# A cross-attention kernel whose hand-written statement order is replaced by another: first rounds, steady round and end

## The chip, the core and the metric

The kernel runs on one core of a Trainium2 chip. The core has a matrix engine (TensorE, PE in the profile, with its weight loads listed as PEld), a vector engine (VectorE, DVE), a scalar engine (ScalarE, ACT), a general engine (GpSimd, POOL) and a queue processor (SyncE, SP) that only issues DMAs here. Each engine takes its instructions in the order in which the program lists them and waits at one until the semaphores that it needs have come. The metric is the device time of one execution in microseconds. Three runs of the kernel before took 1341.26, 1343.85 and 1344.12 us, a median of 1343.85.

## The reference

64 blocks, each of 256 rows of text `x` (width 512) and 256 rows of audio `ctx` (width 384), in float32:

```python
text_p  = einsum('bld,dh->blh', H_l, W_text) + b_text
audio_p = einsum('bsd,dh->bsh', H_a, W_audio) + b_audio
Q = layer_norm(text_p, g1, beta1)
K = layer_norm(audio_p, g2, beta2)
V = audio_p
alpha = softmax(einsum('blh,bsh->bls', Q, K) / sqrt(512))
H_hyper = einsum('bls,bsh->blh', alpha, V)
H_hyper = einsum('blh,hk->blk', H_hyper, W_out) + b_out
return layer_norm(H_hyper + H_l, g_out, beta_out)
```

## The kernel before

All products are float32. To spend fewer products, the kernel uses fast schemes of the Strassen kind: the query projection (class `Fork`, methods `one` to `seven`, 7 products instead of 8), the key projection and the output projection (class `Thirds`, methods `one` to `five`, 15 products of 171 columns), the scores (`score_part`, 7 products) and the context (`z_part`, `context_two`). W_audio and W_out are multiplied together once (`fold_multiply`), so the context is taken over the raw audio rows. These schemes pay with sums of operands, which run on GpSimd and VectorE: `csum` of the audio side (`Sides.add`), `xsum` of the text side (`SumX.add`), `query_step`, `key_step`, `c_step`, `e_step` and `z_step`, and with additions between two products on the accumulators in PSUM (`start_t`, `start_l0`, `start_l1`, `take_m`, `start_u`, `middle_v` and their like on VectorE; `copy_n1`, `copy_t`, `copy_n`, `copy_u`, `after_one`, `after_seven` on ScalarE). A product that needs such a step has to wait for it.

PE contracts over partitions, so operands must be transposed. The kernel transposes 32x32 squares on VectorE (`turn`, line 76, and line 520). For that a matrix is fetched from HBM so that each 32-row strip lies where the transposition wants it: `squares` (line 73) issues four DMAs on SP. x and ctx come from the inputs (`load_x`, `load_c`); normalised queries, keys and the softmax weights are written to a scratch in HBM first (`store` and `store_e`, lines 498 and 931) and fetched back as squares (`fetch` and `fetch_e`), then turned (`turn`, `turn_e`). So each fetch of squares stands between a store and a transposition.

The 64 blocks go through a software pipeline. In round b of the loop, `k2` and `q2` are the key and query projection of block b+2, `at` is the attention of block b (affine of queries and keys, scores, softmax), `last` is the context of block b-1, `old` with `y = old.o` is the output projection of block b-2, `settled` is the final layer norm of block b-3, `cT[b+3]` and `xT[b+3]` are the transposed inputs of block b+3 with their sums, and the loads are for block b+4. The loop runs for b from 3 to 60. Before it stand the first rounds, written out statement by statement with the weights' preparation between them (`third_weights`, `weight_sums`, `turn_weights`, `fold_multiply`), and behind it the end, written out as well, in which the last blocks use plain products (`score`, `context_one`, `multiply`, `multiply_halves`) and the last layer norm is done in halves.

There is no scheduler: `tc.manual_schedule()` leaves the instructions in the order of the statements, which sets the order on every engine's queue and on SP's. Tiles with one buffer (`once`: `kr`, `qr`, `qsum`, `ksum`, `zsum`, `esum`, `asum`, the rooms `n1`, `t`, `m`, `n`, `u`, `d`) and the PSUM banks (`ps_m`, `ps_l`, `ps_u`, `ps_n` for Thirds, two `ps_f` for Fork, two rotating `at` banks for scores and contexts) are written again in each round.

This is the round before (the conditions on b at the last blocks are left out, and the lines that only name things):

```python
k2 = k[b + 2] = Thirds("k", b + 2, cs.pop(b + 2), wa_blocks, ba_sb, ba_delta); old.copy_two(); old.product_sums(); y = old.o; old.z_step(0);
q2.seven(); at.affine_queries(1); old.z_step(7); old.z_step(1); k2.one(); k2.copy_n1(); k2.start_t(); at.affine_queries(0); at.query_sums();
at.query_step(0); load_c(b + 4); q2.six(); at.open_scores(); k2.two(); q2.after_seven(); k2.three(); q2.start_q3(); at.score_part(1, 7); k2.copy_t();
last.fetch_e(); q2.step_r(); k2.start_l1(); k2.start_l0(); q2.five(); old.z_step(2); cT[b + 3] = turn_c(b + 3); at.affine_queries(3); k2.four();
settled.totals(); settled.deviation(0); settled.deviation(1); k[b + 1].turn([0]); settled.last_deviation(); at.copy_p7(); k2.take_m(); k2.start_u();
k2.five(); q2.after_five(); at.affine_queries(2); last.context_sums(); last.c_step(0); q2.four(); at.copy_p1(); settled.shift(1); k2.copy_n();
old.z_step(3); last.c_step(1); k2.copy_u(); k2.leave_ends(); old.z_step(4); cs[b + 3] = Sides(cT.pop(b + 3), "csum").add(0); cs[b + 3].add(1); cs[b +
3].add(1); y.seed(); k2.middle_v(); q2.square(var[:, :2], [1]); k2.leave_middle(); k2.middle_less(); at.query_step(1); old.z_step(5); last.turn_e();
q2.two(); y.one(); settled.shift(0); at.query_step(2); at.score_part(6); k2.leave(); k2.square(var[:, 2:], [1]); y.copy_n1(); old.z_step(6);
q2.three(); y.start_t(); at.add_p7(0); done.store(); done = settled; xT[b + 3] = turn_x(b + 3); y.three(); at.score_part(5); last.weight_sums();
last.e_step(0); last.open_context(); last.z_part(7); at.query_step(3); k2.square(var[:, 2:], [0]); last.e_step(1); y.two(); at.add_p7(1);
at.score_part(2); q2.square(var[:, :2], [0]); cs[b + 3].add(1); y.copy_t(); scales_of(q2, k2, var); at.score_part(3); k[b + 1].turn([1]);
y.start_l1(); last.keep_z7(); q2.normalise([0]); q2.normalise([1]); y.start_l0(); load_x_rows(b - 1); Fork.seed(); last.z_part(1); y.four(); q[b +
1].turn(); x_new = SumX(xT.pop(b + 3)); x_new.add(1); load_c_rows(b); k2.normalise([1]); at.score_part(4); last.e_step(2); settled.settle(1);
last.copy_z1(); k2.normalise([0]); x_new.add(1); last.c_step(2); y.take_m(); last.z_part(6); y.start_u(); att[b + 1] = Attention(b + 1); att[b +
1].affine_keys(0); at.maxima(); y.five(); last.c_step(3); last.add_u3(); cs[b + 3].add(1); settled.settle(0); last.z_part(5); att[b +
1].affine_keys(2); x_new.add(1); load_x(b + 4); last.add_c22(); q3 = q[b + 3] = Fork(b + 3, x_new.of, wt_blocks); q3.one(); x_new.add(1); att[b +
1].affine_keys(1); cs[b + 3].add(1); last.z_part(3); at.exponentials([0]); cs[b + 3].add(1); y.plus_middle(x_old, 1); last.z_part(4);
at.exponentials([1]); y.plus_ends(x_old); q2.store(); y.plus_n0(); att[b + 1].affine_keys(3); at.reciprocals(); att[b + 1].key_sums(); att[b +
1].key_step(0); k2.store(); last.context_two(0); y.last_11(); last.z_part(2); k2.seed(); at.divide_e([0]); q2.fetch(); at.divide_e([1]);
y.plus_middle(x_old, 0); last.copy_top(); y.last_10(); last.context_two(1); k2.fetch(); cs[b + 3].add(1); att[b + 1].key_step(1); y.last_01(x_old);
at.store_e(); last.add_c21(); y.last_00(); q3.after_one(); att[b + 1].key_step(2)
```

Of the kernel before, what the change touches and what calls it, by code (L numbers as in the profile page):

```python
# [22 lines left out]
def kernel(  # L23
# [1289 lines left out]
    war = []  # L1313
    pool, tag = (once, 'e')
    war.append(pool.tile([P, HC, P], F32, tag=tag, name=f'war_{0}'))
    arrange(war[0], wa_sb[:, 0, :], HC, nc.gpsimd.tensor_copy)
# [5 lines left out]
    k[0].multiply(0, [0])  # L1322
    mean_wa = means(wa_sb, AC, 'mwa')
    k[0].multiply(1, [0])
    k[0].multiply(0, [1])
    k[0].multiply(0, [2])
    pool, tag = (work, 'eT')
    war.append(pool.tile([P, HC, P], F32, tag=tag, name=f'war_{1}'))
    arrange(war[1], wa_sb[:, 1, :], HC, nc.gpsimd.tensor_copy)
    pool, tag = (work, 'eT')  # L1330
    war.append(pool.tile([P, HC, P], F32, tag=tag, name=f'war_{2}'))
    arrange(war[2], wa_sb[:, 2, :], HC, nc.gpsimd.tensor_copy)
    x_turn = RowTurn(x_0, DC, 'xT')
    x_turn.tile(0)
    k[0].multiply(1, [1])
    k[0].multiply(1, [2])
    x_turn.tile(1)
    mean_wt = means(wt_sb, DC, 'mwt')
    centre(wa_sb, mean_wa, AC)
    wa_t = const.tile([P, 11, WP], F32, tag='wa_thirds', name='wa_thirds')  # L1340
    third_weights(wa_sb, wa_t, [1], nc.vector)
# [3 lines left out]
    k[0].evict(0)  # L1345
    bt_row = bt_sb.rearrange('p (o h) -> p o h', o=1)
    mean_bt = means(bt_row, 1, 'mbt')
    k[0].evict(1)
    q[0].multiply(1, [0])
    q[0].multiply(1, [1])  # L1350
    q[0].multiply(0, [2])
    cT[1] = turn_c(1)
    q[0].multiply(0, [3])
    q[0].multiply(1, [2])
    q[0].multiply(1, [3])
    centre(bt_row, mean_bt, 1)
    third_weights(wa_sb, wa_t, [0])
    wa_blocks = third_weights(wa_sb, wa_t, [3])
    k[0].scales()
    centre(wt_sb, mean_wt, DC)  # L1360
    k[0].normalise([0])
    k[1] = Projection('k', 1, cT.pop(1), wa_sb, ba_sb, AC, ST, bank[4:6])
    k[1].multiply(0, [0])
    turn_weights(0, 1)
    turn_weights(1, 1)
    xT[1] = turn_x(1)
    q[0].evict(0)
    q[0].evict(1)
    wt_blocks = weight_sums(wt_sb, DC // 2, 'wtsum')
    k[1].multiply(0, [1])  # L1370
    k[1].multiply(0, [2])
    turn_weights(2, 1)
    q[0].scales()
    k[0].normalise([1])
    k[1].multiply(1, [0])
    k[1].multiply(1, [1])
    ba_row = ba_sb.rearrange('p (o h) -> p o h', o=1)
    mean_ba = means(ba_row, 1, 'mba')
    centre(ba_row, mean_ba, 1)
    xs_1 = SumX(xT.pop(1), nc.vector)  # L1380
    xs_1.add(1)
    turn_weights(3, 1)
    fold_multiply(1, 0, 1)
    third_weights(wa_sb, wa_t, [4], nc.vector)
    fold_multiply(0, 0, 1)
    g1_sb, be1_sb, g2_sb, be2_sb, bac_sb = take_columns()
    k[1].multiply(1, [2])
    k[0].store()
    folds.append(p_at.tile([P, H], F32, tag='at', name='ps_fold'))
    fold_multiply(2, 0, 1)  # L1390
    ba_delta = third_bias(ba_sb, 'ba_delta')
    q[0].normalise([0])
    k[1].evict(0)
    Fork.seed()
    fold_multiply(1, 1, 2)
    k[1].evict(1)
    load_c(2)
    fold_multiply(0, 1, 2)
# [3 lines left out]
    q[1].one()  # L1402
    xs_1.add(1)
    bt_step = const.tile([P, H2], F32, tag='bt_step', name='bt_step')
    nc.vector.tensor_tensor(bt_step, bt_sb[:, :H2], bt_sb[:, H2:], ALU.subtract)
    xs_1.add(1)
    load_c(3)
    q[1].seven()
    load_x(2)
    cT[2] = turn_c(2)  # L1410
    k[1].square()
    bias_rest(part, 1, 2)
    k[1].scales()
    fold_multiply(0, 2, 3)
    cs[2] = Sides(cT.pop(2), 'csum')
    cs[2].add(1)
    q[1].after_one()
    q[1].after_seven()
    cs[2].add(1)
    q[1].six()  # L1420
    cs[2].add(1)
    cs[2].add(1)
    q[0].normalise([1])
    q[1].start_q3()
    fold_multiply(0, 3, 4)
    q[1].step_r()
    q[0].store()
    xs_1.add(1)
    fold_multiply(1, 2, 3)
    k[0].fetch()  # L1430
    fold_evict(0)
    q[0].fetch()
    q[1].five()
    load_x(3)
    Thirds.seed_with(ba_sb)
    k[1].normalise([0])
    k[1].normalise([1])
    q[1].after_five()
    cs[2].add(1)
    bias_rest(part, 2, 3)  # L1440
    nc.vector.tensor_scalar(be2_sb, be2_sb, scale, None, ALU.mult)
    cs[2].add(1)
    cs[2].add(1)
    fold_multiply(1, 3, 4)
    bias_rest(part, 3, 4)
    k2_0 = k[2] = Thirds('k', 2, cs.pop(2), wa_blocks, ba_sb, ba_delta)
    k2_0.one()
    k2_0.copy_n1()
    q[1].two()
    k[1].store()  # L1450
    third_weights(wa_sb, wa_t, [2], nc.vector)
    q[1].three()
    k2_0.start_t()
    q[1].four()
# [370 lines left out]
    for b in range(3, B - 3):  # L1825
# [21 lines left out]
        if b + 4 < B: load_c(b + 4)  # L1847
# [503 lines left out]
```

## Time and profile before

| | |
|---|---|
| runs | 1341.26, 1343.85, 1344.12 us |
| profiled execution, own time | 1341.63 us |
| its span, first to last instruction | 1339.8 us |
| instructions | 29994 |
| granted clock of TensorE | 0.999 |
| PE busy | 1329.2 us, 99% |
| DVE busy | 1227.5 us, 92% |
| ACT busy | 1166.9 us, 87% |
| POOL busy | 1152.9 us, 86% |
| DMA | 322.24 MB, mean 241 GB/s |

The span is what the trace covers, and the own time is that of the same execution as the runs are timed, 1.8 us more. A product on PE is listed with the time from its start until its modelled end, while the next one starts earlier, so the distance between starts tells more than the listed time. An entry in brackets behind a row is the engine's idle time before it and what ended it. "SPq" rows are DMA issues; the time is that of the issue, not of the transfer. The chain of work that ended last goes back from the last instruction, at each step to what released it.

### The profile page before, as it was taken

The page shows a single profiled execution, that of the slowest core. Times are in us where ns is not written, and L with a number is a line of the kernel's source. Part 1 is how long each engine was busy: PE and PEld are TensorE (multiplying, and loading weights), DVE is VectorE, ACT ScalarE, POOL GpSimd, SP SyncE. Part 2 cuts the span into 40 slices and gives each one's busy share as a digit, 9 for nine tenths or more (in the row PEclk, how much of TensorE's full clock was granted, in tenths as well). Part 3 has the DMA queues.
Part 4 walks back from the last instruction along what each step waited for, and adds up shares of the span by engine and source line. Part 5 has one row for each costly group of instructions (what it writes and reads, how often), then busy time and mean ns, then how long its engine had stood idle before and what let it go on. Part 6 is the DMA issues. An engine that isn't in the chain of part 4 may idle for free.

```text
span 1339.8 us, 29994 instructions
## 1 busy us (share of the span) xinstructions
PE 1329.2 (99%) x8473; PEld 1246.9 (93%) x8473; DVE 1227.5 (92%) x3308; ACT 1166.9 (87%) x3304; POOL 1152.9 (86%) x1838
## 2 busy tenths in 40 slices
PE   9999999999999999999999999999999999999997
PEld 5899999999999999999999999999999999999996
DVE  6669999999999999999999999999999999999968
ACT  5888888898898888998898898988988988888885
POOL 5768899998998988998998999989989989888854
PEclk9999999999999999999999999999999999999999
DMA  9999898889899888998999888998988898988773
GB/s 213 239 247 237 239 257 242 246 248 243 240 260 250 237 253 245 246 248 234 254 252 237 256 246 241 252 240 244 263 243 241 243 247 238 256 234 247 217 237 109
DMA packets 449115, 322.24 MB, mean 241 GB/s; under 512 B 153781, under 2 KB 381621, under 8 KB 448950
## 3 DMA queue, kind: packets, MB, share of 16 engines
q1 hardware_dynamic: 448854, 320.20, 87.2%
q8 instruction: 68, 1.11, 0.4%
q14 instruction: 97, 0.79, 0.2%
q10 hardware_dynamic: 96, 0.13, 0.0%
HBM read 203.57 MB, written 116.65 MB: 239 GB/s over the span
## 4 chain that ended last, share of the span: by engine, by line
PE 95%; DMA 2%; DVE 1%; ACT 1%; SPq 0%; issue 0%; DVEq 0%; ACTq 0%
PE ps_f L733 27%; PE ps_m L557 16%; PE ps_sc L884 13%; PE ps_n L557 10%; PE ps_u L557 8%; PE ps_z L1000 7%; PE ps_l L557 5%; PE ps_z L1062 5%; PE ps_sc L823 1%; DMA eq<-ed 1%; DMA ed<-e 1%; SPq L73 0%; DMA kq<-kd 0%; PE ps_f L440 0%; DMA beo<-in_L_xattn_beta_out_dram 0%; PE ps_l L244 0%
## 5 line engine op out<-in xcount | busy, mean ns | idle before, releaser
L733 PE MATMUL ps_f<-wtsum,xsum 128*128 128x256 f32 x756 | 193.8, 379 | 0.0
L352 POOL TENSOR_TENSOR csum<-csum,cT 128x256 f32<-128x256 f32 x310 | 173.6, 568 | 5.3
L527 ACT ACTIVATE qT<-qT,columns 128x256 f32<-128x256 f32 x256 | 153.0, 601 | 0.3 <-DVE qT L76 0.3
L733 PEld LDWEIGHTS ps_f<-wtsum,xsum 128*128 128x128 f32 x756 | 136.4, 190 | 14.5 <-issue 1.0
L527 ACT ACTIVATE kT<-kT,columns 128x256 f32<-128x256 f32 x256 | 140.2, 597 | 0.1
L869 POOL TENSOR_TENSOR qsum<-qT 128x256 f32<-128x256 f32 x116 | 110.1, 949 | 31.4 <-ACT qT L527 29.1
L884 PE MATMUL ps_sc<-kT,qT 128*128 128x128 f32 x928 | 131.6, 275 | 0.0
L733 PE MATMUL ps_f<-wt,xT 128*128 128x256 f32 x504 | 129.5, 379 | 0.0
L884 PEld LDWEIGHTS ps_sc<-kT,qT 128*128 128x128 f32 x928 | 122.8, 191 | 0.0
L884 PE MATMUL ps_sc<-ksum,qsum 128*128 128x128 f32 x696 | 105.8, 275 | 0.0
L541 DVE TENSOR_TENSOR ps_l<-ps_m,t 128x171 f32<-128x171 f32 x248 | 85.1, 343 | 20.4 <-ACT t L605 13.2
L733 PEld LDWEIGHTS ps_f<-wt,xT 128*128 128x128 f32 x504 | 91.2, 190 | 10.2 <-issue 0.2
L990 POOL TENSOR_TENSOR esum<-eT 128x256 f32<-128x256 f32 x58 | 62.7, 1080 | 43.9 <-PE ps_n L557 29.7
L794 ACT ACTIVATE junk<-ps_f 128x512 f32<-128x512 f32 x126 | 75.3, 597 | 28.4 <-PE ps_f L733 23.5
L352 POOL TENSOR_TENSOR csum<-cT 128x256 f32<-128x256 f32 x124 | 74.0, 597 | 27.9 <-DVE cT L76 27.2
L314 POOL TENSOR_TENSOR xsum<-xT 128x256 f32<-128x256 f32 x124 | 90.4, 730 | 6.6 <-DVE xT L76 5.2
L884 PEld LDWEIGHTS ps_sc<-ksum,qsum 128*128 128x128 f32 x696 | 95.4, 191 | 0.0
L1125 ACT ACTIVATE junk<-yr,nm 128x512 f32<-128x512 f32 x124 | 88.9, 717 | 6.3 <-POOL nm L1107 0.8
L488 ACT ACTIVATE kr<-kr,rstd 128x512 f32<-128x512 f32 x126 | 91.8, 730 | 0.0
L1261 DVE SCALAR_TENSOR_TENSOR yr<-yr,nm,go 128x512 f32<-128x512 f32 x124 | 91.2, 736 | 0.2 <-ACT junk L1125 0.2
L1270 DVE SCALAR_TENSOR_TENSOR yr<-yr,rstd,beo 128x512 f32<-128x512 f32 x120 | 90.0, 750 | 0.0
L520 DVE STREAM_TRANSPOSE kT<-kq 128x512 f32<-128x512 f32 x122 | 83.7, 687 | 3.4 <-DMA kq<-kd 3.3
(284 smaller groups left out, 4690.0 us busy)
## 6 DMA issues: line engine op xcount, KB each, us to landing
kd<-kr SPq DMA_DIRECT2D x64, 512.0 KB, 3.4
qd<-qr SPq DMA_DIRECT2D x64, 512.0 KB, 3.4
kq<-kd SPq DMA_DIRECT2D x256, 128.0 KB, 3.1
qq<-qd SPq DMA_DIRECT2D x256, 128.0 KB, 2.7
xq<-in_x_dram SPq DMA_DIRECT2D x252, 128.0 KB, 5.7
x<-in_x_dram SPq DMA_DIRECT2D x63, 512.0 KB, 4.9
out_dram<-yr SPq DMA_DIRECT2D x62, 512.0 KB, 3.5
cq<-in_ctx_dram SPq DMA_DIRECT2D x252, 96.0 KB, 3.3
```

Of the source, the lines that this page charges most:

```text
L314: self.engine.tensor_tensor(*step)
L352: nc.gpsimd.tensor_tensor(*step)
L488: nc.scalar.mul(row, row, self.r[t])
L527: nc.scalar.activation(self.T[:, k, :], self.T[:, k, :], AF.Identity, bias=bet[:, k : k + 1], scale=gam[:, k : k + 1],)
L557: nc.tensor.matmul(place, lhsT=self.sides.of[n], rhs=self.weights[n], start=(n == 14), stop=True, skip_group_check=True,)
L733: nc.tensor.matmul(place, lhsT=side, rhs=w, start=(n == 7 and c == 0), stop=True, skip_group_check=True,)
L869: nc.gpsimd.tensor_tensor(*self.steps[n])
L884: nc.tensor.matmul(self.place(t, m), lhsT=self.qsides[n][:, c], rhs=self.ksides[n][:, c], start=False, stop=True, skip_group_check=True,)
L1000: nc.tensor.matmul(self.zp[{1: 0, 2: 0, 4: 2}.get(n, 1)], lhsT=self.asides[n], rhs=self.bsides[n], start=(n == 7), stop=True, skip_group_c ...
L1125: nc.scalar.activation(junk, self.y[:, t, :], AF.Square, bias=self.nm[:, t : t + 1], accum_out=self.ssq[:, t : t + 1],)
L1261: nc.vector.scalar_tensor_tensor(row, row, self.nm[:, t : t + 1], go_sb, ALU.add, ALU.mult)
L1270: nc.vector.scalar_tensor_tensor(self.y[:, t, :], self.y[:, t, :], self.r[t], beo_sb, ALU.mult, ALU.add)
```

## The change

The same statements stand in another order in all three parts: the first rounds, the loop and the end. No statement is added, removed or altered (each of the three parts holds the same set of statements in both kernels), and all classes and helpers are the same. Each fetch of squares from the scratch and its transposition have other places in the round. This is the round of the changed kernel:

```python
k2 = k[b + 2] = Thirds("k", b + 2, cs.pop(b + 2), wa_blocks, ba_sb, ba_delta); old.copy_two(); q2.seven(); at.affine_queries(1); k2.one();
k2.copy_n1(); old.product_sums(); y = old.o; old.z_step(0); last.context_sums(); last.c_step(0); at.affine_queries(0); load_x_rows(b - 1); q2.six();
old.z_step(7); old.z_step(1); k2.start_t(); q2.after_seven(); k2.two(); k2.three(); k2.copy_t(); at.query_sums(); at.query_step(0);
at.affine_queries(2); old.z_step(2); at.open_scores(); q2.start_q3(); q2.step_r(); settled.totals(); at.score_part(1, 7); at.affine_queries(3);
settled.deviation(0); k2.start_l0(); k2.start_l1(); q2.five(); cT[b + 3] = turn_c(b + 3); old.z_step(4); old.z_step(3); at.copy_p7(); last.c_step(1);
at.query_step(1); k2.four(); settled.deviation(1); q2.after_five(); k2.take_m(); cs[b + 3] = Sides(cT.pop(b + 3), "csum").add(0); cs[b + 3].add(1);
settled.last_deviation(); at.copy_p1(); k2.start_u(); k2.five(); settled.shift(1); k2.copy_n(); last.c_step(2); k[b + 1].turn([0]); last.fetch_e();
k2.copy_u(); k2.leave_ends(); y.seed(); last.c_step(3); q2.four(); old.z_step(5); at.query_step(2); q2.square(var[:, :2], [1]); k2.middle_v();
k2.leave_middle(); k2.middle_less(); old.z_step(6); settled.shift(0); last.turn_e(); k2.leave(); cs[b + 3].add(1); q2.two(); k2.square(var[:, 2:],
[0]); y.one(); at.score_part(6); cs[b + 3].add(1); done.store(); done = settled; last.weight_sums(); last.e_step(0); at.add_p7(0); y.copy_n1();
y.start_t(); k2.square(var[:, 2:], [1]); q2.three(); at.score_part(5); xT[b + 3] = turn_x(b + 3); at.add_p7(1); load_c(b + 4); q2.square(var[:, :2],
[0]); y.three(); last.open_context(); last.z_part(7); y.copy_t(); scales_of(q2, k2, var); k[b + 1].turn([1]); y.two(); last.keep_z7(); y.start_l1();
y.start_l0(); settled.settle(1); at.query_step(3); at.score_part(4); q[b + 1].turn(); q2.normalise([0]); at.score_part(3); last.z_part(1);
q2.normalise([1]); last.e_step(1); x_new = SumX(xT.pop(b + 3)); x_new.add(1); last.copy_z1(); x_new.add(1); at.score_part(2); k2.normalise([1]);
load_c_rows(b); y.four(); y.take_m(); y.start_u(); at.maxima(); Fork.seed(); att[b + 1] = Attention(b + 1); att[b + 1].affine_keys(0); load_x(b + 4);
k2.normalise([0]); att[b + 1].affine_keys(3); x_new.add(1); last.z_part(6); cs[b + 3].add(1); att[b + 1].affine_keys(1); at.exponentials([0]);
x_new.add(1); last.add_u3(); y.five(); q2.store(); last.z_part(5); q3 = q[b + 3] = Fork(b + 3, x_new.of, wt_blocks); q3.one(); y.plus_ends(x_old);
last.add_c22(); last.z_part(2); k2.store(); at.exponentials([1]); settled.settle(0); cs[b + 3].add(1); y.plus_middle(x_old, 1); at.reciprocals();
att[b + 1].affine_keys(2); q3.after_one(); cs[b + 3].add(1); y.last_01(x_old); cs[b + 3].add(1); last.z_part(3); at.divide_e([0]); y.plus_n0();
last.e_step(2); last.context_two(0); q2.fetch(); last.z_part(4); y.last_11(); y.last_10(); last.copy_top(); at.divide_e([1]); last.context_two(1);
y.plus_middle(x_old, 0); at.store_e(); k2.fetch(); att[b + 1].key_sums(); att[b + 1].key_step(0); last.add_c21(); y.last_00(); att[b + 1].key_step(1);
att[b + 1].key_step(2); k2.seed()
```

The core of the diff, for the statements of the loop that the text speaks of:

```diff
...
+        load_x_rows(b - 1)
...
-        if b + 4 < B: load_c(b + 4)
         q2.six()
...
-        last.fetch_e()
...
         cT[b + 3] = turn_c(b + 3)
+        old.z_step(4)
+        old.z_step(3)
...
-        k[b + 1].turn([0])
...
+        q2.after_five()
         k2.take_m()
...
         k2.start_u()
         k2.five()
-        q2.after_five()
...
         settled.shift(1)
         k2.copy_n()
+        last.c_step(2)
+        k[b + 1].turn([0])
+        last.fetch_e()
...
+        settled.shift(0)
         last.turn_e()
...
-        settled.shift(0)
...
+        if b + 4 < B: load_c(b + 4)
...
+        at.store_e()
         k2.fetch()
...
-        at.store_e()
```

In the first rounds the statements of the weights' preparation stand elsewhere among the products:

```diff
...
-    beo_sb = row(beta_out, 'beo')
...
+    q[3] = Fork(3, xs.pop(3).of, wt_blocks)
+    q2_1 = q[3]
+    q2_1.one()
     wao_room = const.tile([P, HC * H], F32, tag='wo', name='wao_thirds')
     wao_t = wao_room[:, :11 * WP].rearrange('p (n h) -> p n h', n=11)
     wao_blocks = third_weights(wao_sb, wao_t, [[0, 3], [4, 2]][0])
     cs[4].add(1)
...
+    cs[4].add(1)
...
+    k2_2 = k[4] = Thirds('k', 4, cs.pop(4), wa_blocks, ba_sb, ba_delta)
+    k2_2.one()
...
+    third_weights(wao_sb, wao_t, [1])
+    old_2 = att[0]
...
+    beo_sb = row(beta_out, 'beo')
...
```

And in the end the last steps of the layer norms of the blocks before the last one stand in another order behind the last scores:

```diff
...
     end.maxima()
...
     at.settle(0)
     last.o.plus_n0()
...
     last.shift(0)
-    old.store()
+    last.deviation(1)
+    end.copy_two()
+    at.settle(1)
     end.start_output()
     end.multiply(0, bank[0])
+    last.last_deviation()
+    last.shift(1)
...
     end.multiply_halves(1, bank[1:3])
-    at.settle(1)
...
-    last.shift(1)
...
     end.evict(0, stats=False)
...
```

1333 lines of the change are left out of this document (662 added, 671 removed).

## The prediction

> **What bounds the kernel now.** I read the page's engine shares first, then busy time by stretches, then the chain of work that ended last.
>
> ```profile
> span 1339.8 us, 29994 instructions
> PE 1329.2 (99%) x8473; PEld 1246.9 (93%) x8473; DVE 1227.5 (92%) x3308; ACT 1166.9 (87%) x3304; POOL 1152.9 (86%) x1838
> ```
>
> ```profile
> 604.25:624.55 20.30, 20.30 (x136) 19.47 (x135) 19.29 (x54) 18.16 (x53) 18.37 (x30) 1.00 0.94 246
> ```
>
> The second row is one undisturbed round of the loop (columns: PE, PEld, DVE, ACT, POOL busy, granted clock, DMA share, GB/s). PE is busy for all 20.30 us at clock 1.00, while DVE has 1.01 us of idle time in a round, ACT 2.14, POOL 1.93. No PE instruction is added or removed, so no order can make this round shorter. What can be gained is only what disturbed rounds lose. The chain has one piece per round, q2.four with q2.two behind it:
>
> ```profile
> 103.67 1.73 PE ps_f L733 x8
> ...
> 856.14 1.73 PE ps_f L733 x8
> ...
> 1099.73 1.73 PE ps_f L733 x8
> ...
> 1264.86 1.73 PE ps_f L733 x8
> ...
> 1320.36 0.58 PE ps_n L557 x4
> ```
>
> From 856.14 to 1099.73 lie 12 rounds of 20.30. From 103.67 to 1264.86 lie 57, which at 20.30 are 1157.1; they took 1161.2. So 4.1 us are lost in the loop. The rows also give PE's spacing: 0.865 for a product of Fork, 0.29 for one of Thirds. Such a loss looks like this (timeline of the worst round):
>
> ```profile
> 1134.32 1.88 SPq L73 DMA_DIRECT2D kq<-kd  x4
> 1139.14 0.71 DVE L520 STREAM_TRANSPOSE kT<-kq 128x512 f32<-128x512 f32 x1 [1.03 <-DMA kq<-kd]
> 1140.11 0.34 DVE L541 TENSOR_TENSOR ps_u<-ps_m,m 128x171 f32<-128x171 f32 x1
> 1140.51 0.85 PE L557 MATMUL ps_m<-wa_thirds,cT 128*128 128x171 f32 x4 [0.58 <-DVE ps_u L541]
> 1143.52 0.71 DVE L76 STREAM_TRANSPOSE eT<-eq 128x512 f32<-128x512 f32 x1 [0.54 <-DMA eq<-ed]
> ```
>
> The fetch of kq landed late, DVE stood before the transposition for 1.03 us, start_u behind it came late, and PE stood for 0.58 us in k2.five. Then DVE stood 0.54 us for eq, and what follows on its queue came late as well. Over the whole trace (list of waits: us in total, times, longest):
>
> ```profile
> DVE eT L76 <- DMA eq<-ed: 7.4, 15, 2.1
> DVE kT L520 <- DMA kq<-kd: 3.3, 5, 1.0
> ```
>
> **The change, part by part.** Durations are from this profiled execution: span 1339.84, own time 1341.63, which is 2.2 below the median 1343.85. Nothing is added or removed; each queue is re-ordered. I place the new round against PE at its floor, in offsets from the start of q2.seven, with these rows of an undisturbed round (offset = time - 604.24):
>
> ```profile
> 604.24 1.03 PE L733 MATMUL ps_f<-wtsum,xsum 128*128 128x256 f32 x4
> 604.34 1.88 SPq L73 DMA_DIRECT2D kq<-kd  x4
> 606.33 0.40 SPq L931 DMA_DIRECT2D ed<-e  x1
> 609.47 0.67 DVE L520 STREAM_TRANSPOSE kT<-kq 128x512 f32<-128x512 f32 x1
> 609.59 1.79 SPq L73 DMA_DIRECT2D eq<-ed  x4
> 610.24 0.34 DVE L541 TENSOR_TENSOR m<-ps_m,ba_delta 128x171 f32<-128x171 f32 x1
> 611.20 0.74 DVE L1261 SCALAR_TENSOR_TENSOR yr<-yr,nm,go 128x512 f32<-128x512 f32 x1
> 612.05 0.51 DVE L541 TENSOR_TENSOR kr<-ps_m,n 128x342 f32<-128x342 f32 x1
> 612.27 0.30 ACT L631 COPY u<-ps_u 128x171 f32<-128x171 f32 x1 [0.43 <-PE ps_u L557]
> 612.68 0.33 DVE L541 TENSOR_TENSOR d<-ps_n,u 128x171 f32<-128x171 f32 x1
> 613.16 0.32 DVE L541 TENSOR_TENSOR kr<-d,ps_n 128x171 f32<-128x171 f32 x1
> 613.40 0.70 DVE L76 STREAM_TRANSPOSE eT<-eq 128x512 f32<-128x512 f32 x1
> 613.80 0.74 PE L557 MATMUL ps_n<-wao,zsum 128*128 128x171 f32 x4
> 614.25 1.08 POOL L990 TENSOR_TENSOR esum<-eT 128x256 f32<-128x256 f32 x1 [0.62 <-PE ps_n L557]
> 616.42 0.39 PE L1000 MATMUL ps_z<-esum,asum 128*128 128x128 f32 x2
> ```
>
> *SP's queue.* Before, k2.fetch is issued from offset 0.10 to 1.98 and its transposition starts at 5.23: 3.25 us, against about 3 to land (page, part 6: kq 3.1, ed 3.2, eq 2.1, all medians). store_e is issued at 2.09, fetch_e from 5.35 to 7.14, turn_e at 9.16: 2.02 us against 2.1. Both margins are near nothing, which is why each is missed at times. In the new order store_e moves ahead of k2.fetch, load_x_rows goes between k2.fetch and fetch_e, and load_c goes behind fetch_e. store_e follows divide_e([1]), some 0.5 after the round's start (0.3 to 0.7); behind it k2.fetch is issued from about 1.0 to 2.9; load_x_rows takes 0.5; ed lands at about 3.7 to 4.0 and fetch_e runs to about 5.7. On DVE turn([0]) stands behind start_u and shift(1) now, at 7.3, and turn_e behind shift(0), at 9.95. The distances become 4.4 and 4.2 us instead of 3.25 and 2.02. Even the 1.03 seen above fits. load_x_rows adds 512 KB ahead of eq; a second or so microsecond of queueing still fits in 4.2 - 2.1. load_c, load_x and q2.fetch keep distances above 10 us. I take the 4.1 us in the loop as gained but for 0.5: -3.6.
>
> *DVE's queue, k2.four to y.one.* take_m stays at 6.00 (its input from PE ends then), start_u 0.37 later. Then shift(1) (0.66 to the next start), turn([0]) (0.67), leave_ends (0.43) bring DVE to 8.38, where middle_v, leave_middle and middle_less follow; before, DVE reached middle_v at 8.44. copy_u ends at 8.33, so that is the same place. middle_less ends at 9.24, y.one starts at 9.56 in both orders: 0.3 to spare, as before (an instruction on DVE starts some 0.08 before the recorded end of the one ahead, which is where 0.66 and 0.43 come from, out of 0.74 and 0.51). after_five and z_step(4), (3), moved ahead of take_m, fill the place that turn([0]) had. Change: 0.
>
> *turn_e to z_part(7).* turn_e moves from 9.16 to 9.95, so e_step(0) on POOL can start at 10.8; e_step(0) takes 1.08 at most, and z_part(7) stands at 12.18 (row 616.42), as before. What was 1.1 us to spare becomes 0.3 or more. add_p7(0) waits for score_part(6), which PE ends at about 10.6 by the count of its products, so DVE is in step with PE again there. start_t ends at 11.3 for y.three at 11.89, more room than before. Change: 0.
>
> *The rest of the round.* qT, take_m and start_u of y fall to 15.7 and 16.1, y.five needs start_u at 16.77. ACT runs without a pause from copy_t of y to copy_two at about 0.5 of the next round, behind the same last product as before. POOL has key_step up to 1.5, and query_step(0) at 2.5. Change: 0.
>
> *First rounds.* Before, PE waited for the first turn_e, whose fetch stood behind the row of beta_out on SP:
>
> ```profile
> 63.72 4.44 DMA beo<-in_L_xattn_beta_out_dram
> 68.17 3.53 DMA eq<-ed
> 72.50 1.99 PE ps_z L1062 x8
> ```
>
> The change loads that row later: -0.3. Against it, thirds of W_out (nine POOL additions of some 0.5) now stand ahead of two csum steps that k2_2.one waits for; by my count they end within 0.3 us of need. W_out itself lands as before, and PE reaches its first use as early. Bounds -1.0 and +2.0; I take +0.5 in sum, nearer the row above than a whole missed step.
>
> *End.* The last PE product decides, and the DVE steps behind it are the same:
>
> ```profile
> 1330.12 0.75 DVE L1168 SCALAR_TENSOR_TENSOR y<-ps_m,rden,x 128x512 f32<-128x512 f32 x1 [0.16 <-PE ps_m L1159]
> ```
>
> at.settle(1) and last.shift(1) now reach DVE with (my estimate from the rows of these forms) 11.5 us of work from end.maxima on, which PE releases at about 1319.0, so that the last evict could start at 1330.5 instead of 1330.12: bounds 0 and +0.6, taken +0.2.
>
> Sum: 1341.63 - 3.6 + 0.5 - 0.3 + 0.2 = 1338.4. The runs of before that took 1344 lose, as I read it, more of the same DMA lateness, so I compare this with the median as it is: 0.4% below 1343.85.
>
> **A lock between DVE and POOL.** In the trace the same DVE form takes very different times:
>
> ```profile
> L1261 DVE SCALAR_TENSOR_TENSOR yr<-yr,nm,go x124: 703/740/1300, 102.7 to 1329.2; 128x512 f32<-128x512 f32 x124
> L1270 DVE SCALAR_TENSOR_TENSOR yr<-yr,rstd,beo x120: 707/742/1025, 111.3 to 1314.2; 128x512 f32<-128x512 f32 x120
> ```
>
> and esum above took 1.08 while shift(0) ran beside it. The Trainium skill (SBUF — State Buffer, "Who interferes with whom") has a rule for this: a DVE instruction with two SBUF inputs and a GpSimd instruction that reads SBUF exclude each other for the whole instruction, and the one that starts first wins. The trace agrees as to the length (up to 1300 against 703). If a shift or settle falls into the middle of a POOL step, DVE loses up to 0.6 us. Before, the four of a round start where POOL is idle or nearly through, hence the median of 740. By my placing shift(1) at 6.62 meets c_step(3) at 6.67 within 0.05 us, settle(1) at 13.9 meets a POOL change at 13.98, shift(0) the last tenth of a csum step, settle(0) an idle POOL.
>
> **Rivals.**
> - *The lock decides (slower).* DVE loses 0.3 at shift(1) (1040-like, between 703 and 1300) and up to 0.6 at settle(1), where y.five has 0.36 to spare. From that point on each round pays the excess: 0.15 us, with 0.05 and 0.3 as ends, times 58 rounds, 3 to 17 us; 1338.4 + 8.7 = 1347.1. For it: DVE's idle share is only 1.01 per round, and POOL is busy 90%. Against it: a lost 0.3 still leaves y.one in time, and DVE falls in step at add_p7(0) and plus_ends.
> - *DMA lateness stays (no change).* At a DMA share of 0.94 the waits may come from the sum of traffic, which is the same; fetch_e then waits behind load_x_rows. The 3.6 are not gained: 1342.0, and with worse first rounds 1343.5. Against it: distances grow by 1.2 and 2.2 us, more than nearly all waits.
> - *First rounds or end stall (smaller gain).* Two missed steps of about 1.5: 1341.
>
> **How the numbers follow.** Forecast 1338.4, chance 0.56, own range 1335.8 (all 4.1 gained, first rounds -1.0) to 1340.8. Lock: 0.20. DMA lateness stays: 0.14. First rounds or end: 0.10. 0.2% of 1343.85 is 2.7, about what a measurement can tell: faster means below 1341.2. The forecast and half of the third rival give 0.61; within 0.2% 0.20; slower, above 1346.5, most of the lock's upper part and what I overlooked, 0.19. The range goes from 1335.6 to 1348.0, so that the lock's middle value is in.
>
> **What would show it.** Right: the round's period in the chain is 20.30 throughout; the waits of DVE for eq and kq are gone or below 1 us in sum; shift and settle keep medians near 740. Lock: L1261 or L1270 with a median above 850 and rounds above 20.30 by a constant. DMA: waits for eq or kq persist. First rounds: the loop's first q2.four later than 103.5. Wrong would be any new constant wait of PE in each round, of k2.five or y.one for DVE above all.

## The result and the profile after: slower, by a lock that the forecast priced too low

The changed kernel takes 1357.42 us (median of 4, 1356.27 to 1358.03), the kernel before 1343.24 beside it: ratio 1.0107, 95% interval 1.0089 to 1.0124. Forecast were 1338.4, a range of 1335.6 to 1348.0, and a chance of 0.19 for slower. The page of the changed kernel:

```profile
span 1355.6 us, 29587 instructions
PE 1343.8 (99%) x8473; PEld 1240.2 (91%) x8473; DVE 1266.0 (93%) x3308; ACT 1181.1 (87%) x3304; POOL 1105.2 (82%) x1838
```

Against the page before, DVE is busy for 38.5 us more and POOL for 47.7 us less, with the same number of instructions on each engine (the 407 fewer of the first line are semaphore instructions, which are not counted as busy). The chain of waits of the changed kernel, q2.four of five rounds (start, us):

```profile
310.71 1.73 PE ps_f L733 x8
331.34 1.73 PE ps_f L733 x8
351.97 1.73 PE ps_f L733 x8
372.26 1.73 PE ps_f L733 x8
392.89 1.73 PE ps_f L733 x8
```

Three of the four rounds take 20.63 instead of 20.30, one takes 20.29. A usual round and the exceptional one, by stretches (columns: stretch, length, then PE, PEld, DVE, ACT, POOL busy, clock, DMA share, GB/s):

```profile
499.98:520.60 20.62, 20.62 (x135) 19.32 (x135) 20.03 (x54) 18.41 (x53) 17.44 (x30) 1.00 0.88 251
340.50:360.80 20.30, 20.30 (x136) 19.47 (x136) 19.59 (x54) 18.38 (x53) 18.28 (x31) 1.00 0.90 247
```

In the usual round DVE works 0.74 longer than the 19.29 of before and POOL 0.93 less than its 18.37; their sum hardly moves. The two DVE forms of the lock (min/median/max ns):

```profile
L1261 DVE SCALAR_TENSOR_TENSOR yr<-yr,nm,go x124: 711/1037/1756, 102.8 to 1344.3; 128x512 f32<-128x512 f32 x124
L1270 DVE SCALAR_TENSOR_TENSOR yr<-yr,rstd,beo x120: 741/744/1160, 110.4 to 1332.8; 128x512 f32<-128x512 f32 x120
```

shift (L1261) has gone from a median of 740 to 1037. Where it happens, in the timeline of the usual round (DVE and POOL rows: settle(1), shift(1), shift(0)):

```profile
502.39 1.02 DVE L1270 SCALAR_TENSOR_TENSOR yr<-yr,rstd,beo 128x512 f32<-128x512 f32 x1
514.95 0.46 POOL L987 TENSOR_TENSOR asum<-asum,c 128x128 f32<-128x128 f32 x1
515.45 1.04 DVE L1261 SCALAR_TENSOR_TENSOR yr<-yr,nm,go 128x512 f32<-128x512 f32 x1
515.48 0.45 POOL L987 TENSOR_TENSOR c<-c,asum 128x128 f32<-128x128 f32 x1
515.89 0.90 POOL L1051 TENSOR_TENSOR zsum<-zsum,zT 128x128 f32<-128x128 f32 x1
518.25 0.72 POOL L352 TENSOR_TENSOR csum<-csum,cT 128x256 f32<-128x256 f32 x1
518.35 1.17 DVE L1261 SCALAR_TENSOR_TENSOR yr<-yr,nm,go 128x512 f32<-128x512 f32 x1
```

and of the round of 20.29:

```profile
350.60 0.74 DVE L1261 SCALAR_TENSOR_TENSOR yr<-yr,nm,go 128x512 f32<-128x512 f32 x1
350.64 1.02 POOL L987 TENSOR_TENSOR c<-c,asum 128x128 f32<-128x128 f32 x1
```

In the usual round shift(1) starts 30 ns ahead of c_step(3) (c<-c,asum) and loses: it ends 0.55 behind the end of that POOL step (515.94 to 516.49). In the exceptional round it starts 40 ns ahead and wins; c_step(3) takes 1.02 instead of 0.45. All 162 long shifts and settles of this trace (over 0.8 us) end 0.54 to 0.55 behind the end of a POOL step. In the kernel before shift(1) meets a POOL step in 54 rounds too, but starts 0.12 ahead of it in the median, and it is POOL that pays: 1.20 in the round below instead of 0.73.

```profile
407.87 0.74 DVE L1261 SCALAR_TENSOR_TENSOR yr<-yr,nm,go 128x512 f32<-128x512 f32 x1
408.00 1.20 POOL L869 TENSOR_TENSOR qsum<-qT 128x256 f32<-128x256 f32 x1 [0.16 <-ACT qT L527]
```

In the changed kernel a usual round loses 1.04 + 1.17 + 1.02 - 3 x 0.74 = 1.0 us of DVE time; POOL, which does not pay, runs early and meets shift(0) and settle(1) too.

The trace adds up so. PE's time beyond the usual spacing of its products (the median distance to the next start, for each form of product in the trace of before, summed over all rows) goes from 4.0 to 4.3 up to 110 us, from 4.2 to 18.3 between 110 and 1262, from 0.6 to 0.9 behind that, and what follows the last product from 7.2 to 8.3. These make the 15.8 by which the span grew; the loop has 14.1 of them. DVE lost shift(1) in 53 rounds, and 53 x 0.33 = 17.5 of the 18.3. The 0.8 that is left stands against the 4.2 of before, which the prediction puts down to DMA lateness. (An expectation below counts 2.4 and 16.6 for the loop; the difference is the same.)

The DMA part did nearly what was forecast (waits of the changed kernel):

```profile
DVE kT L520 <- DMA kq<-kd: 1.6, 1, 1.6
DVE eT L76 <- DMA eq<-ed: 1.4, 2, 1.0
PEld ps_sc L884 <- DVE ps_sc L541: 15.7, 53, 0.5
```

Waits for kq and eq fell from 10.7 us in 20 places to 3.0 in 3; below 1 was the forecast sign. In their place stands a wait in each of 53 rounds: score_part(5) of PE for add_p7(0) on DVE, which stands behind shift(0) and turn_e. By the distances between the starts of products, PE loses about 0.16 of the 0.33 there, 0.07 at y.one, behind shift(1), and 0.08 at y.five, behind settle(1).

### The profile page after: what moved, and what is told of

Read it like the earlier page. It is cut to its first block, busy times and chain, and to the rows that moved or that the text cites. A ratio compares the mean times of both kernels' runs of the same rounds, so it can differ in the third digit from the quotient of the medians.

```text
span 1355.6 us, 29587 instructions
## 1 busy us (share of the span) xinstructions
PE 1343.8 (99%) x8473; PEld 1240.2 (91%) x8473; DVE 1266.0 (93%) x3308; ACT 1181.1 (87%) x3304; POOL 1105.2 (82%) x1838
## 4 chain that ended last, share of the span: by engine, by line
PE 97%; DVE 1%; DMA 1%; ACT 0%; issue 0%; SPq 0%; POOL 0%; DVEq 0%; POOLq 0%
PE ps_f L733 28%; PE ps_m L557 16%; PE ps_sc L884 14%; PE ps_n L557 11%; PE ps_u L557 8%; PE ps_z L1000 7%; PE ps_l L557 5%; PE ps_z L1062 5%; PE ps_sc L823 2%; DMA eq<-ed 0%; PE ps_f L440 0%; DVE yr L1261 0%; DMA c<-in_ctx_dram 0%; PE ps_l L244 0%; PE ps_u L440 0%
## 5 line engine op out<-in xcount | busy, mean ns | idle before, releaser
L527 ACT ACTIVATE qT<-qT,columns 128x256 f32<-128x256 f32 x256 | 147.6, 602 | 0.5 <-DVE qT L76 0.5
L527 ACT ACTIVATE kT<-kT,columns 128x256 f32<-128x256 f32 x256 | 147.4, 602 | 0.0
L1261 DVE SCALAR_TENSOR_TENSOR yr<-yr,nm,go 128x512 f32<-128x512 f32 x124 | 131.6, 1062 | 0.0
L884 PEld LDWEIGHTS ps_sc<-kT,qT 128*128 128x128 f32 x928 | 119.3, 191 | 1.0
L869 POOL TENSOR_TENSOR qsum<-qT 128x256 f32<-128x256 f32 x116 | 84.6, 729 | 40.4 <-ACT qT L527 40.4
L866 POOL TENSOR_TENSOR ksum<-kT 128x512 f32<-128x512 f32 x58 | 74.0, 1276 | 52.1 <-ACT kT L527 52.1
L884 PE MATMUL ps_sc<-ksum,qsum 128*128 128x128 f32 x696 | 111.4, 283 | 0.1
L1270 DVE SCALAR_TENSOR_TENSOR yr<-yr,rstd,beo 128x512 f32<-128x512 f32 x120 | 103.9, 866 | 0.0
L990 POOL TENSOR_TENSOR esum<-eT 128x256 f32<-128x256 f32 x58 | 42.2, 728 | 72.1 <-DVE eT L76 69.8
L1062 PE MATMUL ps_z<-eT,c 128*128 128x256 f32 x304 | 86.7, 380 | 0.6 <-PE ps_u L557 0.6
```

The lines of the kernel that those rows point to most:

```text
L527: nc.scalar.activation(self.T[:, k, :], self.T[:, k, :], AF.Identity, bias=bet[:, k : k + 1], scale=gam[:, k : k + 1],)
L884: nc.tensor.matmul(self.place(t, m), lhsT=self.qsides[n][:, c], rhs=self.ksides[n][:, c], start=False, stop=True, skip_group_check=True,)
L1062: nc.tensor.matmul(ps, lhsT=c_rows[self.b][:, s, bass.ts(j, P)], rhs=self.eT[:, s, :], start=start, stop=(s == ST - 1), skip_group_check=True,
L1261: nc.vector.scalar_tensor_tensor(row, row, self.nm[:, t : t + 1], go_sb, ALU.add, ALU.mult)
L1270: nc.vector.scalar_tensor_tensor(self.y[:, t, :], self.y[:, t, :], self.r[t], beo_sb, ALU.mult, ALU.add)
```

## Experiments

Theory 1: the lock between DVE and POOL, decided by who is first, makes the rounds longer. Theory 2: the new order on DVE is too late by itself. The runs were made on several chips; the kernel before took 1351 to 1353 on four of them and 1343.5 on one, so each ratio is against the runs of the kernel before beside it.

**A short fill ahead of c_step(3).**

```
+        nc.gpsimd.memset(pause, 0.0)      # pause: 128x32
         last.c_step(3)
```

> The changed kernel with one tiny POOL instruction more in each round (a fill of 128x32 ahead of c_step(3)), nothing else. In the changed kernel shift(1) starts on DVE at 515.45 and c_step(3) on POOL at 515.48, and DVE takes 1036 ns; in the one round in which POOL was 40 ns behind DVE (350.60 against 350.64), DVE took 741. Theory 1 (the lock, decided by who is first): with POOL a little later DVE wins in every round, shift(1) and shift(0) take about 1.49 us together instead of 2.21, c_step(3) takes about 1.0 instead of 0.45, the round is 20.30 instead of 20.63 and the kernel about 1340 (1357.4 less 52 rounds of 0.33), between 1338 and 1342. Theory 2 (the order on DVE itself brings add_p7(0) too late for score_part(5), lock or no lock): L1261 gets shorter but the rounds stay at 20.5 or more, 1350 or more. Theory 3 (POOL is short of time): longer by up to 58 times the fill, 1360 or more.

Measured: 1356.56, ratio 1.0040 (1.0020 to 1.0060): nothing gained. A round of it, POOL and DVE:

```profile
534.77 0.46 POOL L987 TENSOR_TENSOR asum<-asum,c 128x128 f32<-128x128 f32 x1
535.16 0.13 POOL L1892 MEMSET pause<- 128x32 f32 x1
535.28 1.03 DVE L1261 SCALAR_TENSOR_TENSOR yr<-yr,nm,go 128x512 f32<-128x512 f32 x1
535.31 0.46 POOL L987 TENSOR_TENSOR c<-c,asum 128x128 f32<-128x128 f32 x1
```

c_step(3) depends on c_step(2) and in the changed kernel stands 80 ns behind its end anyway. The fill used that gap up, and c_step(3) was still only 30 ns behind. The experiment missed its aim and separates nothing, but for some rounds in which DVE won and which took 20.30.

**c_step(2) earlier on POOL.**

```
+        last.c_step(2)
         at.query_step(1)
...
-        last.c_step(2)
```

> The changed kernel with c_step(2) moved on POOL alone to ahead of query_step(1). POOL has 0.2 us idle there, so that its step boundary falls some 0.25 behind the start of shift(1) instead of 0.05 ahead of it: a csum step runs when shift(1) starts and has 0.2 to 0.3 us left. Theory 1 (the lock): shift(1) ends about 0.55 behind the end of that step, 0.75 to 0.85 us instead of 1.04; the POOL steps behind it wait for DVE, as in the round at 350 us, so shift(0) and settle(1) are near 740 too; rounds of 20.30 to 20.40, kernel 1340 to 1346. If shift(0) still meets the middle of a csum step, 1.1 us there and rounds of 20.45 or more, 1349 or more. Theory 2 (order on DVE alone): no change, 1357.

Measured: 1350.08, ratio 0.9970 (0.9948 to 0.9992), the best of this group of four. The round and its places:

```profile
411.08:431.51 20.43, 20.43 (x136) 19.40 (x135) 19.70 (x54) 18.27 (x52) 17.41 (x30) 1.00 0.91 248
```

```profile
409.39 0.45 POOL L987 TENSOR_TENSOR c<-c,asum 128x128 f32<-128x128 f32 x1
409.72 1.09 DVE L1261 SCALAR_TENSOR_TENSOR yr<-yr,nm,go 128x512 f32<-128x512 f32 x1
409.81 0.45 POOL L1051 TENSOR_TENSOR zsum<-zsum,zT 128x128 f32<-128x128 f32 x1
```

shift(1) still loses, by another way than I thought: it starts in the last 0.13 of c_step(3), and z_step(5) behind it takes the lock without a gap, though DVE stood there 90 ns before. But shift(0) falls to 0.76 and settle(1) to 0.86. With 0.5 lost instead of 1.0 the round is 20.43 instead of 20.63; PE loses the 0.13 at y.one, and score_part(5) is not late. The order of DVE is that of the changed kernel, so theory 2 alone does not explain the rounds.

**The lock put into the kernel before.** An exchange of neighbours on DVE:

```
-        settled.shift(1)
         k2.copy_n()
         old.z_step(3)
+        settled.shift(1)
```

> The kernel before, with one exchange of neighbours on DVE in the loop: shift(1) behind z_step(3) instead of two statements ahead of it. In the kernel before shift(1) starts at 407.87 and query_step of POOL at 408.00, so DVE wins (740) and POOL pays (1198 instead of 730). Starting 0.2 later DVE comes second. Theory 1a (the lock, and a single loss on the path to y.one is passed on): shift(1) takes 1.2 instead of 0.74, POOL's step 0.73; y.one had about 0.3 to spare, so some 0.15 a round, 57 rounds, 1343.2 + 9 = 1352 (1348 to 1358). Theory 1b (the lock, but only DVE's sum counts, which has 1.01 idle in a round): the same long shift(1), rounds of 20.30, 1343. Without the lock (theory 2) shift(1) stays at 740 and the time at 1343.

Measured: 1360.97, ratio 1.0065 (1.0038 to 1.0092). One round, from the timeline:

```profile
413.93 0.72 POOL L869 TENSOR_TENSOR qsum<-qT 128x256 f32<-128x256 f32 x1 [0.15 <-ACT qT L527]
414.01 1.20 DVE L1261 SCALAR_TENSOR_TENSOR yr<-yr,nm,go 128x512 f32<-128x512 f32 x1
415.66 0.45 ACT L571 COPY ps_m<-bao 128x342 f32<-128x342 f32 x1 [0.47 <-DVE kr L541]
416.23 0.32 DVE L541 TENSOR_TENSOR kr<-d,ps_n 128x171 f32<-128x171 f32 x1
416.66 0.59 PEld L557 LDWEIGHTS ps_n<-wao,zsum 128*128 128x128 f32 x4 [0.49 <-ACT ps_m L571]
```

shift(1) is long as expected, and the round is 20.65 (the stretch 414.85 to 435.50 between two q2.four). A single loss of 0.46 is passed on but for 0.1, more than the 0.15 a round that was expected. The path is shift(1), then the DVE steps behind it without a pause down to middle_less (kr<-d,ps_n), then y.one, which may write ps_n only when middle_less has read it. The bracket of the last row names y.seed on ACT (ps_m<-bao), but that had ended at 416.11, 0.55 earlier, and y.one does not touch ps_m. middle_less ends at 416.55, and the first weight load of y.one starts 0.11 behind it. This distance is the same, 0.11 to 0.12, in every measured round of this run and of the kernel before: there, too, the weight load had no time to spare. What was spare is that the product then starts 0.20 behind its weight load, and only 0.03 behind it when the load comes late; standing costs 0.08 again between the products of y.one, which leaves 0.1. The sum of DVE's idle time does not matter (theory 1b falls); what matters is the spare time of this path.

**Loop and borders exchanged.** h1 has the loop of the changed kernel between the first rounds and end of the kernel before; h2 the opposite. The kernel before to h1, at the loop's head:

```
     for b in range(3, B - 3):
...
         old.copy_two()
-        old.product_sums()
-        y = old.o
-        old.z_step(0)
         q2.seven()
         at.affine_queries(1)
...
```

> First rounds and end of the kernel before, the loop of the changed one. If the loop alone carries the loss (PE's lost time between 110 and 1262 us is 16.6 in the changed kernel and 2.4 before): 1343.2 + 14 = 1357, rounds of 20.63. If the state in which the first rounds leave POOL and DVE decides who is first at shift(1): rounds of 20.30 and 1338 to 1341. If first rounds and end carry it: within 3 of 1343.

> The opposite exchange: first rounds and end of the changed kernel, the loop of the one before. If first rounds and end are worth as little as the traces say (start +0.3, last DVE steps +1.1): 0 to 2 us above the kernel before on the same chip. More than 4 above: they, or the state that they leave, count.

h1: 1359.25, ratio 1.0051 (1.0033 to 1.0069), rounds of 20.62, long shifts. h2: 1354.66, ratio 1.0008 (0.9985 to 1.0031), median shift 740. The loop carries the loss; first rounds and end are within the measurement. The state in which the first rounds leave the engines does not decide: the lock sets in either way.

**A long fill ahead of c_step(3).** As the first, with a wider tile:

```
-    pause = const.tile([P, 32], F32, tag='pause', name='pause')
+    pause = const.tile([P, 128], F32, tag='pause', name='pause')
```

> As the first run, but the POOL instruction put ahead of c_step(3) fills 128x128 instead of 128x32. The short one took 127 ns and filled only the 80 ns that c_step(3) stood anyway behind c_step(2), on whose result it depends: in most rounds c_step(3) still started 20 to 30 ns behind shift(1) and won; in the rounds in which it started 40 or more behind, DVE took 742. The long fill takes about 204 ns (the fill of ident at the start of the kernel has that form and time), so that c_step(3) starts about 0.1 us behind shift(1) in every round. Lock, decided by who is first: shift(1) and shift(0) at 740 in nearly all rounds, settle(1) at 745, rounds of 20.30, some 15 us below the first run: 1339 to 1343. If DVE standing in the lock does not come first (POOL's instructions follow each other without a gap): shift(1) 1.0 or more and 1355 or more.

Measured: 1360.35, ratio 1.0049 (1.0029 to 1.0070). A round:

```profile
515.64 0.20 POOL L1892 MEMSET pause<- 128x128 f32 x1
515.75 1.05 DVE L1261 SCALAR_TENSOR_TENSOR yr<-yr,nm,go 128x512 f32<-128x512 f32 x1
515.80 0.45 POOL L987 TENSOR_TENSOR c<-c,asum 128x128 f32<-128x128 f32 x1
```

DVE starts 50 ns ahead of c_step(3) and still loses, in all rounds but one, in which it started 91 ns ahead. So "who is recorded first" is too simple. Where POOL's instructions follow without a gap DVE needs more: in the second run 90 ns are not enough either.

**The short fill ahead of c_step(2)**, with the gap ahead of c_step(3) left alone, and the changed kernel beside it:

```
+        nc.gpsimd.memset(pause, 0.0)      # pause: 128x32
         last.c_step(2)
```

> The changed kernel with the short fill (128x32, 127 ns) in another place of POOL's queue: ahead of c_step(2) instead of c_step(3). What the first two runs with a fill taught: where the instruction of POOL that runs as DVE starts is followed by the next without a gap, DVE is not let in between (1054 with the long fill, although DVE started 50 ns ahead of c_step(3)). c_step(3) depends on c_step(2) and stands 80 ns behind it in every round, so there is a gap; in the changed kernel shift(1) starts 30 ns ahead of its end and is too late. With c_step(2) ending some 0.09 later shift(1) starts about 0.12 ahead of c_step(3), as it does ahead of its POOL step in the kernel before. Lock, with the gap: shift(1) and shift(0) at 740, c_step(3) at about 0.95, settle(1) at 745, rounds of 20.30, 1339 to 1344, and faster than the kernel before. If DVE loses here too, or rounds stay at 20.5 or more with L1261 at 740: the lock is not what makes the round longer, and DVE's order is; 1352 or more.

> The changed kernel itself, on the same chip as the run above, for the comparison: 1356 to 1360, rounds of 20.63, a spread of runs of some 3 us, whatever the kernel before takes on this chip, since its waits for eq and kq are gone. If the chip that made the kernel before slow makes this one slow too: 1365 or more.

Measured: 1340.98 with the fill (ratio 0.9903, 0.9882 to 0.9924), 1358.85 without (1.0051, 1.0030 to 1.0072). An added instruction of 0.12 us takes 17.9 us off, as 53 x 0.33 had it. One round of the kernel with the fill, and its places:

```profile
490.09:510.39 20.30, 20.30 (x136) 19.48 (x135) 19.39 (x54) 18.35 (x52) 17.97 (x31) 1.00 0.89 245
```

```profile
508.50 0.12 POOL L1886 MEMSET pause<- 128x32 f32 x1
508.57 0.46 POOL L987 TENSOR_TENSOR asum<-asum,c 128x128 f32<-128x128 f32 x1
509.02 0.74 DVE L1261 SCALAR_TENSOR_TENSOR yr<-yr,nm,go 128x512 f32<-128x512 f32 x1
509.11 0.97 POOL L987 TENSOR_TENSOR c<-c,asum 128x128 f32<-128x128 f32 x1
```

DVE starts 90 ns ahead of c_step(3), with the gap in between, and wins; shift(0) and settle(1) follow at 0.74 to 0.75. DVE's order is untouched, the rounds are 20.30: theory 2 falls, theory 1 stands.

**The same without a fill.** Of the two steps of totals() on POOL the second goes behind query_step(1) (totals takes the rows as an argument):

```
-        settled.totals()
+        settled.totals([0])
...
         at.query_step(1)
+        settled.totals([1])
```

> The changed kernel, nothing added and no fill: of the two small steps of totals() on POOL (264 ns each), the second goes behind query_step(1). POOL stands 0.2 us ahead of query_step(1) for ACT, so that the step in its old place delays nothing behind; in the new place csum, c_step(2) and c_step(3) start some 0.23 later. ACT needs its result for deviation(1), 0.26 later than now. c_step(2) then ends about 0.2 behind the start of shift(1), and the gap of 80 ns ahead of c_step(3) follows. Lock, with the gap: shift(1) 0.72 to 0.8, shift(0) 0.74, rounds of 20.30 and 1340 to 1343 as with the fill ahead of c_step(2), so faster than the changed kernel by 15 or more and faster than the kernel before. If the fill did something else than shift c_step(3) behind shift(1): 1352 or more. If ACT's later deviation(1) is passed on: rounds of 20.4 or more with L1261 at 740.

Measured: 1341.31, ratio 0.9926 (0.9899 to 0.9953). Stretch of a round, and shift(1):

```profile
490.00:510.30 20.30, 20.30 (x136) 19.48 (x136) 19.34 (x54) 18.34 (x53) 17.79 (x30) 1.00 0.96 256
```

```profile
509.34 0.74 DVE L1262 SCALAR_TENSOR_TENSOR yr<-yr,nm,go 128x512 f32<-128x512 f32 x1
509.60 0.79 POOL L987 TENSOR_TENSOR c<-c,asum 128x128 f32<-128x128 f32 x1
```

No work is added. The kernel before took 1353.03 beside it; the changed kernel was not run on this chip, and took 1357.42 and 1358.85 on two others. On a chip on which the kernel before takes 1343 this version was not run.

**The kernel before on another chip, and the order on SP.** First a profile of the kernel before where it takes 1353:

> The kernel before itself, for a profile from the chip on which it took 1351 (1345 to 1364) instead of 1343. If DMA lateness makes that spread: waits of DVE for eq and kq of 15 us or more in sum instead of 10.7, rounds of 20.30 between them and L1261 at 740. If it is the lock: L1261 or L1270 long in many rounds.

```profile
DVE eT L76 <- DMA eq<-ed: 14.0, 27, 1.7
DVE kT L520 <- DMA kq<-kd: 8.8, 11, 1.8
```

The median is 1353.06, the shifts stay at 740, and the waits for eq and kq are 22.8 us instead of 10.7. PE's lost time in the loop, counted as above, is 13.7 instead of 4.2, nearly the 9.8 us between the two profiled executions: what makes the kernel before slower on this chip is DMA lateness. The changed order keeps 2.9 to 5.8 us of these waits in the runs on such chips. Then load_c ahead of fetch_e, on SP alone, once in the kernel with the long fill and once in the version with the second step of totals() moved:

```
+        if b + 4 < B: load_c(b + 4)
         last.fetch_e()
...
-        if b + 4 < B: load_c(b + 4)
```

> The kernel of the run before with one more change, on SP alone: load_c(b+4) goes ahead of fetch_e, as in the kernel before. The issue of fetch_e then ends some 1.9 us later, about 2 us ahead of turn_e instead of 4 to 5. If the distance between fetch and transposition is what keeps DMA lateness out: waits of DVE for eq come back (7.4 us in sum in the first profile of the kernel before, none in the changed kernel), the time rises by 2 to 8 us over the run before it and its runs spread over 5 us or more, as those of the kernel before do. If the DMA waits depended on total traffic only: the same time as without this edit, within 1.5.

> The kernel of the run before (second step of totals() behind query_step(1), 1341.31, no long shift) with load_c(b+4) ahead of fetch_e on SP, the edit that cost 27 us while DVE lost in the lock. Distance theory: fetch_e's issue ends about 2.3 us ahead of turn_e instead of 4 to 5, and waits of DVE for eq come back. If a wait is passed on only as far as DVE has no idle time left (20.03 of 20.62 us busy with the lock, 19.34 of 20.30 without): part of the waits is absorbed, 1344 to 1356, more or less what the kernel before takes. If every wait is passed on whatever DVE's idle time: 1360 or more, as with the lock. If DMA waits depend on total traffic alone: 1341, within 1.5.

Measured: 1387.65 (1.0251, 1.0220 to 1.0282) and 1385.22 (1.0304, 1.0278 to 1.0330), 27 us above the kernel without the edit beside it, and 44 above the other, which ran on another chip. The first expectation (2 to 8 us) was far too low; of the second, the branch came true in which every wait is passed on (1360 or more). The waits of the second, and one round of its SP queue and of DVE and PE:

```profile
DVE eT L76 <- DMA eq<-ed: 58.3, 55, 2.5
```

```profile
710.04 0.40 SPq L97 DMA_DIRECT2D x<-in_x_dram  x1
710.48 1.95 SPq L73 DMA_DIRECT2D cq<-in_ctx_dram  x4
712.48 4.23 SPq L73 DMA_DIRECT2D eq<-ed  x4
719.47 0.71 DVE L76 STREAM_TRANSPOSE eT<-eq 128x512 f32<-128x512 f32 x1 [2.46 <-DMA eq<-ed]
720.42 0.71 PE L884 MATMUL ps_sc<-ksum,qsum 128*128 128x128 f32 x4 [1.84 <-DVE ps_sc L541]
```

Total traffic is the same, so the DMA rival of the prediction (waits from the sum of traffic) falls. The wait of this round fits the distance: the issues of fetch_e end at 716.71, 0.3 ahead of the time at which DVE is free for turn_e (717.01), and turn_e starts 2.76 behind them. What no expectation had is how short the distance becomes: with the rows of x and the squares of c ahead of them, the four issues take 4.23 on SP instead of the 1.79 of before. Why they stretch is not shown by these runs. The lateness also brings the lock back at another place: shift(1) stays at 0.75, but settle(1) now meets a POOL step and takes 1.02 in 55 rounds, and PE loses 0.08 at y.five in 49 of them, about 4 us.

## Why the prediction was wrong, point by point

- **SP's queue (-3.6): right in kind.** Waits for kq and eq went from 10.7 to 3.0 here, and are 2.9 to 5.8 in the versions with the changed order on chips where the kernel before takes 1351 to 1353. In the loop that is about -3.4 (4.2 before, 0.8 beside the lock).
- **DVE's queue, k2.four to y.one ("Change: 0"): wrong, by the lock; this is the step that failed.** I saw that shift(1) "meets c_step(3) at 6.67 within 0.05 us" and let it be decided for DVE in the forecast. It is 30 ns, and DVE loses 0.3 there in 53 of 58 rounds. The step also has 0.3 to spare between the end of middle_less and y.one; the weight load of y.one follows middle_less by 0.11 already in the kernel before, and the spare time is 0.1.
- **"shift(0) the last tenth of a csum step": wrong as a consequence.** That was placed with POOL paying at shift(1). POOL did not pay, ran half a microsecond earlier, and shift(0) starts 0.10 into a step of 0.72. In the rounds in which shift(1) wins, shift(0) meets the last 0.17 of the csum step ahead of that one, much as forecast, and takes 0.74. settle(1) met its POOL step (+0.28), settle(0) an idle POOL, as said. That in the kernel before the four "start where POOL is idle or nearly through" misses half of it: at shift(1) POOL's next step came 0.13 behind and was held.
- **The lock as a rival (chance 0.20, 1347.1): right mechanism, term too small.** Its price was 0.15 a round between 0.05 and 0.3; measured are 0.33. Two steps of its argument failed. "A lost 0.3 still leaves y.one in time" measured to the start of the product; the third experiment shows 0.1 to spare, because the weight load ahead of it waits for middle_less. "DVE falls in step at add_p7(0)" had the direction wrong: PE's score_part(5) waits for add_p7(0).
- **First rounds (+0.2 in sum): right, as far as it can be told**; the time that PE lost up to 110 us grew by 0.3, but other traces of the same first rounds have 3.2 to 5.0 us there, so the hit is no more than luck.
- **End (+0.2, bounds 0 and +0.6): wrong, +1.3**, by the lock again. last.shift(1) starts 0.12 behind a POOL step of 1.33 and takes 1.76 instead of 0.74; the evict behind it starts 3.97 instead of 2.85 behind the start of its PE group:

```profile
1344.14 1.33 POOL L1279 TENSOR_TENSOR yr<-yr,beo 128x512 f32<-128x512 f32 x1 [0.58 <-ACT yr L1275]
1344.26 1.76 DVE L1261 SCALAR_TENSOR_TENSOR yr<-yr,nm,go 128x512 f32<-128x512 f32 x1
1345.94 0.74 DVE L1168 SCALAR_TENSOR_TENSOR y<-ps_m,rden,x 128x512 f32<-128x512 f32 x1
```

- **The sum without the lock: nearly right.** The profiled execution of the version with the second step of totals() moved takes 1340.61, against 1338.4; the end makes 1.1 of that difference. So the forecast was a good one for another kernel, in which c_step(3) on POOL is 0.1 to 0.2 us later. The lower end of its own range does not follow from its terms: 1338.4 - 0.5 - 1.5 - 0.2 is 1336.2, not 1335.8.
- **The chances.** A coin lay on its edge by my own placing (0.05 us), in every round alike. Such an outcome deserved a chance near one half, and a price up to the part of the loss that the path to PE cannot take up (0.33 a round, as measured), not 0.20 and the mean.

## What to carry to other kernels

When two engines exclude each other, a re-ordering moves not only work but also who pays. Before, POOL paid, and the rounds stayed at 20.30; after, DVE paid, on a path to PE with 0.1 us to spare. In a loop such a meeting repeats in every round with the same few tens of nanoseconds, so look for DVE instructions of this kind that start just beside a POOL boundary, list which engine came second there, and shift the one with time to spare on its path until it is the one that waits. Measure the spare time ahead of a product to its first weight load, not to the product. And where a profile names a releaser that had ended long before, look for another: here a constant distance to the end of another instruction gave it away.

## What was not expected of the hardware

- The lock has a sharp border, and it does not lie at zero by the recorded starts. In the changed kernel (two traces), in h1 and with the short fill ahead of c_step(3), c_step(3) stands 20 to 80 ns behind the POOL instruction ahead of it. Of the rounds in which the two start beside each other DVE won shift(1) in 23, with a lead of 37 to 78 ns, and lost it in 201, with 37 ns or less. Where POOL's instructions follow without a gap DVE needs more: it lost with 40 to 58 ns of lead behind the long fill and won once with 91, and it lost with 79 to 97 in 54 rounds of the run with c_step(2) earlier.
- The Trainium skill (SBUF — State Buffer, "Who interferes with whom") has it that a DVE instruction with two SBUF inputs contends with a GpSimd instruction that reads SBUF, and that issue order decides who blocks. The trace agrees with the block for the whole instruction (long ones end 0.54 to 0.56 behind the POOL step); who is first cannot be read from recorded starts alone to within about 0.1 us.
- No round inherits the lock from the one before: in the changed kernel each of the four rounds in which DVE won shift(1), 10 ns or less beyond the usual lead in three of them, took 20.30, and the next one was long again.
- One load moved ahead of a fetch on SP costs 27 us beside the same kernel without it, and 44 in a comparison across two chips, without a byte more of traffic.
- The kernel before varies between chips (1343 to 1353), with its DMA waits for eq and kq (10.7 and 22.8 us in one trace each). The changed one took 1357.42 and 1358.85 on two.
